# Layer 0 of a four-layer network on Trainium2: other operands and other engines for some of its work

## The chip, the cores and the metric

The kernel runs on one core of a Trainium2 chip. A core has a matrix engine (TensorE, PE in the profile, with its weight loads shown apart as PEld), three engines for elementwise work (VectorE or DVE, ScalarE or ACT, GpSimd or POOL), and SyncE (SP), which here only issues transfers. Each engine works through its own list of instructions in order and waits at semaphores for the others. Data lie in an on-chip memory (SBUF) of 128 partitions, in eight banks of an accumulation memory (PSUM), which PE writes, and in DRAM, which only DMA transfers reach. The metric is the device time of one execution of the whole program, in microseconds (us).

## The reference

Four layers are applied to an image x of 1 x 1024 channels x 64 x 64 pixels in float32, each as x + layer(groupnorm(x)). Layers 1 and 3 are 1x1 convolutions, layer 2 is a larger block with a selective scan. The change concerns layer 0 alone:

```
x_norm = layernorm2d(_gn(x), ln_w, ln_b)          # per channel, over 64 x 64 pixels
A_cont = -exp(log_A)                              # one per image row, 64
dt     = softplus(einsum('bsdc,c->bsd', x_norm, dt_w[0]) + dt_b[0])
log_a  = dt * A_cont                              # (channel s, image row d)
cums   = cumsum(log_a, axis=1)
M      = exp(cums[t] - cums[j]) for t >= j, else 0
out    = einsum('btjr,bjrc->btrc', M, x_norm)     # x = x + out
```

The channels are the sequence. For each channel and image row there is one dt: a weighted sum over the 64 pixels of that row. With a = exp(dt·A_cont), `out` is the recurrence out[t] = a[t]·out[t−1] + x_norm[t] along the 1024 channels, for every pixel, with one a for all pixels of an image row.

## The kernel before

**Tiles.** The image has channels on partitions when it arrives: 8 channel tiles of 128 x 4096 pixels. Layer 0 takes them in four pairs (`CH` = 2 channel tiles), and each pair in two halves of 32 image rows; that makes `NU` = 8 units. Unit u is pair u // 2, half u % 2. A unit is split into four pieces (`NPIECE`), so there are `NI` = 32 pieces. A piece is 512 pixels of the two channel tiles. In the turned layout, in which the recurrence runs, a tile has 128 pixels on the partitions (32 image rows x `TW` = 4 pixels) and the 256 channels of the pair along the free axis; a unit has `T0` = 16 such tiles, a piece has 4 of them.

**One unit's way.** `norm_chunk` works out mean and variance of a pair of channel tiles. `normalize(n)` (L580 to L587) makes a tile of 128 channels x 1024 pixels on ACT, with scale and bias per channel; there are 32 of them, four per unit, two of which feed two pieces. They have two buffers for each channel tile. `turn_in(i)` (L594 to L610) turns a piece: PE transposes (L602) into PSUM, and DVE (L608) or ACT (L610) writes it from there to `XT[i]` with the layernorm's weights. `row_dt(i)` (L612 to L618) adds the piece's part to the unit's row sums: the weights `dtm[:, t, :]` are stationary and the turned pixels move, so that PSUM gets the row sum of every pixel's row on all 128 partitions, as 128 x 256 channels. `decay(u, 0)` works out softplus on ACT (L627 to L630), as max(v, 0) + ln(1 + exp(−|v|)), in two tiles; `decay(u, 1)` adds the two by identity matmuls (L633); `decay(u, 2)` takes exp with the scale A to get the decays (L637 for the first channel, L638 for the others, spread over two tiles). `begin(u)` (L641 to L646), on POOL, adds what the last channel pair of the same half left to the first channel of the unit. `scan(i)` (L653) is the recurrence on DVE, two instructions of 512 for a piece. `hand_on(i)` (L658), on POOL, keeps the last channel. `turn_back(i)` turns a piece back (PE transposes, L679), and `add_up(i)` adds it to the image on DVE (L692), which also gives the sums for the next layer's statistics. Where `by_act(i, k)` holds (L660: pieces 25 to 30, second channel tile), PE adds the image itself by an identity matmul (L671, and products L677 in place of the transposes), and ACT copies the sum out (L690). `squares` (L704) gives the sums of squares on ACT.

**The order.** The whole layer is issued under a manual schedule: each engine gets its instructions in the order in which the program issues them. In the main loop, step i issues: the normalize of tile i+9, `decay(u+1, 1)` in the third step of a unit, `scan(i)`, `hand_on(i)`, `add_up(i−1)`, `turn_in(i+7)` (`LEAD` = 7), `row_dt(i+6)`, `turn_back(i)`, in a unit's second step `decay(u+1, 0)`, in its third `decay(u+1, 2)` and `begin(u+1)`, then pieces of the statistics, squares, a store of half the finished pair (`keep`, 2 MB, at steps 4, 12, 20, 28), the load of the last unit pair's first half at step 5 (`bring(6)`), and one turn of `sums`.

**The sums.** `sums` is work for later layers: `sum_weights` (L442 to L462) makes sums and differences of blocks of the two next weight matrices, in eight chunks. Chunk c loads four tiles of 256 KB (L450) at step 4c, does four POOL operations of 128x512 (L456 to L459) at step 4c+2, and stores four tiles (L462) at step 4c+3. Its transfers are issued by POOL, on its own DMA queue. The image's loads, the keeps and the weights of layer 1 are issued by SP.

Of the kernel before, what the change touches and what calls it, by code (L numbers as in the profile page):

```python
# [10 lines left out]
F32 = mybir.dt.float32  # L11
# [3 lines left out]
AF = mybir.ActivationFunctionType  # L15
ALU = mybir.AluOpType
# [4 lines left out]
P = 128  # L21
# [16 lines left out]
NK = -(-N // LT)  # L38
# [8 lines left out]
W1, WX, WR, WG, WO, W3 = range(6)  # L47
# [18 lines left out]
T0 = HN // P  # L66
TR = HW // 2
TW = HW // T0
# [6 lines left out]
        ("Alog", S), ("D", 1), ("mob", 4 * HEADS), ("dbcb", HEADS * NF)]  # L75

_CST = [("ident", P), ("fold", LC), ("same", P), ("upto", LC), ("far", LC), ("eye", LC), ("eye8", S),
        ("from", 1), ("to", NK), ("group", P), ("row", P),
        ("gx", NT), ("gy", NT), ("flip", 7)]


# [13 lines left out]
def tile_net(ctx: ExitStack, tc: tile.TileContext, x, par_d, cst_d, w_d, w2_d, dbcw_d, out):  # L95
# [28 lines left out]
    def pcol(name, i, rows=P):  # L124
        at = PAR[name].start + i
        return par[:rows, at : at + 1]
# [384 lines left out]
    with tc.issue_after(exp_ln.ins), tc.tile_pool(name="l0x", bufs=2) as lx, \  # L511
# [32 lines left out]
        nc.scalar.activation(negA0, par[:, PAR["logA"]], AF.Exp)  # L544
        negA = const.tile([P, S], F32, name="negA")
        nc.scalar.activation(negA, par[:, PAR["Alog"]], AF.Exp)
        dtm = l0.tile([P, T0, P], F32, name="dtm", bufs=1)
        for t in range(T0):
            nc.gpsimd.tensor_scalar(dtm[:, t, :], cst[:, CST["row"]], pcol("dtw", t), None, ALU.mult)
        carry = l0.tile([P, 2, T0], F32, name="carry", bufs=1)  # L550
# [29 lines left out]
        def normalize(n):  # L580

            u, j = divmod(n, 4)
            q, k = divmod(j, CH)
            scale, bias = norms[u // 2]
            xn[n] = l0.tile([P, 2, TR, HW // 4], F32, tag=f"xn{k}", name=f"xn{n}")
            part = half(u)[:, k, :].rearrange("p (r a g w) -> p a g r w", r=TR, a=2, g=2)[:, q]
            nc.scalar.activation(xn[n], part, AF.Identity, bias=bias[:, k : k + 1], scale=scale[:, k : k + 1])  # L587

        def tile_in(u, t, k):
            v = xn[4 * u + CH * (t // 8) + k].rearrange("p g r w -> p (g r w)")  # L590
# [21 lines left out]
        def row_dt(i):  # L612
            u, g = divmod(i, NPIECE)
            if g == 0:
                PD[u] = ps0.tile([P, FB], F32, tag="pd", name=f"pd{u}")
            for j in range(4):
                t = 4 * g + j
                nc.tensor.matmul(PD[u][:, : CH * P], dtm[:, t, :], XT[i][:, j, :], start=(t == 0), stop=(t == T0 - 1))  # L618

        def decay(u, step):  # L620

            if step == 0:
                e = l0.tile([P, CH * P], F32, tag="e", name=f"e{u}", bufs=1)
                m = l0.tile([P, CH * P], F32, tag="m", name=f"m{u}", bufs=1)
                dt[u] = e, m
                v = PD[u][:, : CH * P]
                nc.scalar.activation(e, v, AF.Abs, bias=pcol("dtb", 0))  # L627
                nc.scalar.activation(e, e, AF.Exp, scale=-1.0)
                nc.scalar.activation(m, v, AF.Relu, bias=pcol("dtb", 0))
                nc.scalar.activation(e, e, AF.Ln, bias=1.0)  # L630
            elif step == 1:
                for i, v in enumerate(dt[u]):
                    nc.tensor.matmul(PD[u][:, CH * P :], ident, v, start=(i == 0), stop=(i == 1))  # L633
            else:
                v, scale = PD[u][:, CH * P :], negA0[:, u % 2 : u % 2 + 1]
                if u > 1:
                    nc.scalar.activation(first_[u % 2], v[:, :1], AF.Exp, scale=scale)  # L637
                nc.scalar.activation(spread[u % 2][:, :, 1:], v[:, 1:].unsqueeze(1).to_broadcast([P, 2, CH * P - 1]),  # L638
                                     AF.Exp, scale=scale)
# [18 lines left out]
                nc.gpsimd.tensor_copy(carry[:, u % 2, 4 * g : 4 * g + 4], XT[i][:, :, CH * P - 1])  # L658

        def by_act(i, k):  # L660
            return NI - LEAD <= i < NI - 1 and k == 1

        def pieces_of(i, k):
            u, g = divmod(i, NPIECE)
# [38 lines left out]
                junk = junk[:, :FB].rearrange("p (r w) -> p r w", r=TR)  # L703
            nc.scalar.activation(junk, part, AF.Square, bias=nmean0[:, ct : ct + 1], accum_out=sq0[:, ct, at : at + 1])  # L704

        sums = (None for m in (W1, WX) for _ in sum_weights(m, wsum0, nc.gpsimd, lag=(1, 0)))
        LEAD = 7
        scores = make_scores()
        for k in range(CH):
# [34 lines left out]
                later[i] = [pieces.pop(0) for _ in range(n)]  # L744
        for i in range(NI):
            u, g = divmod(i, NPIECE)
            if i > 1 and i + LEAD + 2 < 4 * NU:
                normalize(i + LEAD + 2)
            if u + 1 < NU and g == 2:
                decay(u + 1, 1)  # L750
            scan(i)
            hand_on(i)
            if i == 0:
                finish_of(chain)
                chain = iter(())
            if i > 0:
                add_up(i - 1)
            if i == 0:
                turn_in(5, (2, 3))
                turn_back(0)  # L760
                turn_in(6, (2, 3))
                row_dt(5)
            elif i + LEAD < NI:
                if i == 1:
                    row_dt(LEAD - 1)
                    turn_in(LEAD, (2, 3))
                    normalize(LEAD + 3)
                turn_in(i + LEAD, (2, 3) if i > 11 and i % 2 else ())
            if 0 < i <= NI - LEAD:
                row_dt(i + LEAD - 1)  # L770
            if i > 0:
                turn_back(i)
            if i == 0:
                normalize(LEAD + 1)
                normalize(LEAD + 2)
            if u + 1 < NU and g == 1:
                decay(u + 1, 0)
            if u + 1 < NU and g == 2:
                decay(u + 1, 2)
                if u > 0:  # L780
                    begin(u + 1)
            for v, n in later.get(i, ()):
                unit_stats(v, (n,))
            if i in (3, 11):
                chain = norm_chunk(2 if i == 3 else 3)
            next(chain, None)
            if i >= NPIECE and g < CH:
                squares(u - 1, g)
            if u == NU - 1 and 0 < g:
                for k in range(CH):  # L790
                    squares(u, k, g - 1)
            if g == 0 and u % 2 == 1:
                last_keep = keep(u // 2)
            if i == NPIECE + 1:
                bring(6)
            next(sums, None)
# [1014 lines left out]
def _constants():  # L1811
    c = np.zeros((P, NCST), np.float32)
    p, j = np.arange(P)[:, None], np.arange(P)[None, :]
    c[:, CST["ident"]] = p == j
    h, r = np.divmod(p, LC)
    t = np.arange(LC)[None, :]
    c[:, CST["fold"]] = r == t
    c[:, CST["same"]] = h == j // LC
    c[:, CST["upto"]] = (t < S) | (r <= t)
    c[:, CST["far"]] = np.where((r >= S) & (t >= S) & (t < r), FAR, 0)  # L1820
    c[:, CST["eye"]] = (r == t) & (r >= S)
    c[:KW, CST["eye8"]] = np.tile(np.eye(S), (KW // S, 1))
    c[:, CST["from"]] = HEADS * N + np.where(r < S, h * S + r, HEADS * S)
    c[:, CST["to"]] = HEADS * N + np.arange(NK)[None, :] * P + p
    c[:, CST["group"]] = (p // 32 == j // 32) / 32
    c[:, CST["row"]] = p // TW == j // TW
    s = 1 - 2 * ((np.arange(P)[:, None] >> np.arange(6)[None, :]) & 1)
    s[:, 5] = 1
    c[:, CST["flip"]] = np.concatenate([s[:, :1], -s[:, :1], s[:, :5] * s[:, 1:]], axis=1)
    lin = _side()  # L1830
    c[:, CST["gx"]] = np.tile(lin, HW).reshape(NT, P).T
    c[:, CST["gy"]] = np.repeat(lin, HW).reshape(NT, P).T
    return c
# [63 lines left out]
```

## Time and profile before

| What | us |
|---|---|
| median of 3 runs | 2649.37 (2644.72 to 2649.58) |
| the profiled execution | 2649.3 |
| its span | 2647.4 |
| layer 0's steps 0 to 31, roughly | 42 to 203 |
| first matmul of layer 1 (L880) | 202.5 |
| one step while PE is without a gap (147 to 155 us) | 3.56 |

The mean clock that TensorE was granted is 0.993 of full speed. The profile's page gives busy time by engine; the trace behind it was asked for four stretches of layer 0, for what PE waited for, and for timelines. In a timeline a row has its start, its duration, the engine, the line of the program, the operation with output and inputs, the shape, the count of equal instructions in a row, and, in brackets, the idle time before it and what ended that. Since matmuls overlap, the distance between two starts tells more of PE's pace than the duration of a row.

### The profile page before, as it was taken

How to read it: one execution, taken by the hardware profiler on the slowest of the kernel's cores; microseconds unless marked ns; L12 is line 12 of the kernel's file. 1: busy time of each engine (PE TensorE's matmuls, PEld its weight loads, DVE VectorE, ACT ScalarE, POOL GpSimd, SP SyncE). 2: the span in 40 equal slices, each digit the busy share in tenths (PEclk: the TensorE clock that was granted, in tenths of full speed). 3: DMA queues.
4: the chain of work that ended last, by engine and by line, in shares of the span. 5: the costliest groups of instructions: out<-in, count | busy, mean ns of one | idle time of the engine just before them, and what ended most of it. 6: DMA issues, size and time to landing. Idle time of an engine off the chain costs nothing.

```text
span 2647.4 us, 30728 instructions
## 1 busy us (share of the span) xinstructions
PE 2561.7 (97%) x9588; PEld 1715.7 (65%) x9588; DVE 1817.3 (69%) x3794; ACT 1073.6 (41%) x1807; POOL 1225.4 (46%) x1142
## 2 busy tenths in 40 slices
PE   5889999999999999999999999999999999899998
PEld 4774444444555555544454548888888888788887
DVE  7986775674565554377877766576585775877877
ACT  4882110104655544476767662332233223312120
POOL 2464214322324142246464735575565665554544
PEclk9999999999999999999999999999999999999999
DMA  6555648656655676587677847899899898888896
GB/s 247 191 186 179 217 162 269 211 147 208 191 146 142 159 180 167 171 259 223 201 237 233 294 141 211 221 275 292 234 294 255 248 305 222 274 294 300 296 325 215
DMA packets 422772, 597.22 MB, mean 226 GB/s; under 512 B 142004, under 2 KB 210739, under 8 KB 419540
## 3 DMA queue, kind: packets, MB, share of 16 engines
q1 hardware_dynamic: 298052, 367.89, 44.4%
q10 hardware_dynamic: 91456, 136.33, 14.6%
q0 software_dynamic: 33104, 91.04, 13.5%
q8 instruction: 78, 1.28, 0.2%
q14 instruction: 82, 0.67, 0.1%
HBM read 435.10 MB, written 160.05 MB: 225 GB/s over the span
## 4 chain that ended last, share of the span: by engine, by line
PE 84%; DVE 6%; ACT 6%; DMA 1%; issue 1%; POOL 1%; SPq 0%; DVEq 0%; ACTq 0%; POOLq 0%
PE mm L880 38%; PE q_P2P L1771 5%; PE q_P6P L1771 5%; PE q_P5P L1771 5%; PE q_P3P L1771 5%; PE q_P7P L1771 5%; PE q_P4P L1771 5%; PE q_P1P L1771 5%; PE l2pt L1133 2%; PE py L1418 2%; ACT b L984 1%; DVE cvp L1114 1%; PE pd L618 1%; DVE xt L653 1%; PE pr L1379 1%
## 5 line engine op out<-in xcount | busy, mean ns | idle before, releaser
L880 PE MATMUL mm<-t,w 128*128 128x512 f32 x1536 | 681.4, 594 | 0.0
L880 PE MATMUL mm<-b,w 128*128 128x512 f32 x1152 | 513.2, 596 | 4.0 <-ACT b L984 2.9
L880 PEld LDWEIGHTS mm<-t,w 128*128 128x128 f32 x1536 | 286.0, 190 | 321.6 <-issue 314.6
L880 PEld LDWEIGHTS mm<-b,w 128*128 128x128 f32 x1152 | 215.4, 191 | 251.3 <-issue 239.0
L1427 POOL DMA_INDIRECT y_rows<-g,dst x74 | 73.6, 994 | 184.0 <-ACT g L1423 170.4
L1114 DVE SCALAR_TENSOR_TENSOR cvp<-xs,par,cvp 128x512 f32<-128x512 f32 x128 | 95.3, 754 | 78.9 <-ACT cvp L1111 76.7
L1740 ACT COPY qQ<-q_P5P 128x512 f32<-128x512 f32 x48 | 28.1, 585 | 294.0 <-PE q_P5P L1771 241.5
L470 POOL TENSOR_TENSOR s<-s 128x256 f32<-128x256 f32 (+3 forms) x120 | 130.2, 1090 | 7.5
L1421 ACT COPY g<-py 8x512 f32<-8x512 f32 x146 | 83.9, 575 | 107.4 <-PE py L1418 103.8
L1165 DVE TENSOR_TENSOR xs<-mm,xs 128x512 f32<-128x512 f32 x64 | 41.8, 685 | 119.0 <-PE mm L880 119.0
L1141 POOL TENSOR_TENSOR acc<-l2xt,acc 128x136 f32<-128x136 f32 x56 | 29.2, 522 | 193.6 <-ACT l2xt L1135 186.5
L1001 DVE SCALAR_TENSOR_TENSOR image<-mm,par,image 128x512 f32<-128x512 f32 x64 | 47.1, 746 | 87.7 <-PE mm L880 87.7
L1133 PEld LDWEIGHTS l2pt<-both,cv 128*128 128x128 f32 x512 | 77.4, 192 | 35.1 <-issue 22.7
L984 ACT ACTIVATE b<-image,gnl_bias,gnl_r_r 128x512 f32<-128x512 f32 x48 | 36.9, 808 | 144.1 <-PE mm L880 130.3
L1539 ACT ACTIVATE qb<-x_x_b,gn_bias,gn_r_r 128x512 f32<-128x512 f32 x64 | 48.8, 807 | 112.0 <-DVE qQ L1701 47.9
L1771 PE MATMUL q_P4P<-t_t,wq_P4P 128*128 128x256 f32 x384 | 92.5, 384 | 1.4 <-DVE qV L1748 1.4
L1771 PE MATMUL q_P1P<-t_b,wq_P1P 128*128 128x256 f32 x384 | 91.5, 382 | 1.5 <-POOL t_b L1535 1.5
L1535 POOL TENSOR_TENSOR t_t<-qt 128x512 f32<-128x512 f32 x23 | 29.6, 1288 | 135.9 <-DVE qt L1535 76.1
L838 POOL TENSOR_TENSOR t<-t,b 128x512 f32<-128x512 f32 x40 | 55.7, 1420 | 78.2 <-DVE t L838 78.1
L1748 DVE TENSOR_TENSOR qV<-q_P4P,qV 128x512 f32<-128x512 f32 x96 | 64.9, 686 | 38.7 <-PE q_P4P L1771 37.0
L1771 PE MATMUL q_P5P<-t_t,wq_P5P 128*128 128x256 f32 x384 | 90.8, 379 | 0.0
L1771 PE MATMUL q_P6P<-t_t,wq_P6P 128*128 128x256 f32 x384 | 90.7, 379 | 0.0
(433 smaller groups left out, 5991.4 us busy)
## 6 DMA issues: line engine op xcount, KB each, us to landing
w<-s_d SPq DMA_DIRECT2D x96, 512.0 KB
w<-in_w_dram SPq DMA_DIRECT2D x72, 512.0 KB
x_x_b<-x_d ACTq DMA_DIRECT2D x28, 1024.0 KB
image<-x_d SPq DMA_DIRECT2D x12, 2048.0 KB
wq_P6P<-s_d SPq DMA_DIRECT2D x84, 256.0 KB
wq_P7P<-s_d SPq DMA_DIRECT2D x84, 256.0 KB
wq_P5P<-s_d SPq DMA_DIRECT2D x84, 256.0 KB
wq_P3P<-s_d SPq DMA_DIRECT2D x84, 256.0 KB
```

What stands on the lines that cost most here:

```text
L470: eng.tensor_tensor(out, a, b, ALU.subtract)
L838: eng.tensor_tensor(B[name][k], B[one][k], B[two][k], ALU.subtract)
L880: nc.tensor.matmul(to[o], w[:, k, o * P : (o + 1) * P], B[name][k], start=(fresh and k == 0), stop=(k == KH - 1), skip_group_check=True)
L984: nc.scalar.activation(t, X[nb][:, ct, :], AF.Identity, bias=bias, scale=scale)
L1114: nc.vector.scalar_tensor_tensor(cv, xo[:, at + t : at + t + FB], pcol("dww", 3 * o + t), cv, ALU.mult, ALU.add)
L1133: nc.tensor.matmul(pt[:, q * NV : (q + 1) * NV], cv[:, (q0 + q) * P : (q0 + q + 1) * P], both[:, o, :], start=True, stop=True)
L1418: nc.tensor.matmul(py, G2[k % 2], rows[k][:, :DH], start=True, stop=True)
L1421: nc.scalar.copy(rows[k + 1][h * LC : h * LC + S, :DH], py[h * LC : h * LC + S])
L1427: nc.gpsimd.indirect_dma_start(out=y_views[k % len(y_views)][:, :], out_offset=bass.IndirectOffsetOnAxis(ap=dst_[:, k : k + 1], axis=0), i ...
L1539: nc.scalar.activation(tile_of(j, name)[:, k], held[j, "x", name][:, k], AF.Identity, bias=bias, scale=scale)
L1748: nc.vector.tensor_tensor(to, ps, to, ALU.add)
L1771: nc.tensor.matmul(ps[:, o, :], w[:, k, o * P : (o + 1) * P], rhs[:, k, :], start=(new and o == 0 and k == 0), stop=(k == 1), skip_group_c ...
```

## The change

Six things are changed, all in layer 0.

1. `row_dt`: the turned pixels are the stationary operand now, in two blocks of 128 channels, and `dtm`, which has 32 columns (one for each image row) in place of 128, moves. A piece has eight matmuls of 32 columns in place of four of 256. PSUM gets channels on the partitions and image rows along the free axis, 128 x 64 for a unit.
2. `decay`: |v| and exp work on 128 x 64; max(v, 0) and ln write 128 x 256, with each row's value repeated for its four pixels. `decay(u, 1)` adds the two parts and turns them to pixels on partitions in the same matmuls, four of 128 columns in place of two of 256.
3. `normalize` runs on POOL from tile 11 on (21 of 32 tiles), as one tensor_scalar with a multiplication and an addition; ACT keeps the first 11. In the loop they are issued in pairs at odd steps.
4. The sums' transfers are issued by SP in place of POOL.
5. `by_act` holds for pieces 4 to 13 too.
6. `turn_in` at odd steps from 13 on writes all four tiles by ACT; before, DVE wrote two of them.

```diff
-        ("from", 1), ("to", NK), ("group", P), ("row", P),
+        ("from", 1), ("to", NK), ("group", P), ("row", TR),
...
-        dtm = l0.tile([P, T0, P], F32, name="dtm", bufs=1)
+        dtm = l0.tile([P, T0, TR], F32, name="dtm", bufs=1)
...
-            nc.scalar.activation(xn[n], part, AF.Identity, bias=bias[:, k : k + 1], scale=scale[:, k : k + 1])
+            scale, bias = scale[:, k : k + 1], bias[:, k : k + 1]
+            if n > LEAD + 3:
+                nc.gpsimd.tensor_scalar(xn[n], part, scale, bias, ALU.mult, ALU.add)
+            else:
+                nc.scalar.activation(xn[n], part, AF.Identity, bias=bias, scale=scale)
...
-                nc.tensor.matmul(PD[u][:, : CH * P], dtm[:, t, :], XT[i][:, j, :], start=(t == 0), stop=(t == T0 - 1))
+                for k in range(CH):
+                    nc.tensor.matmul(PD[u][:, k * TR : (k + 1) * TR], XT[i][:, j, k * P : (k + 1) * P], dtm[:, t, :],
+                                     start=(t == 0 and k == 0), stop=(t == T0 - 1), skip_group_check=True)
...
-                e = l0.tile([P, CH * P], F32, tag="e", name=f"e{u}", bufs=1)
-                m = l0.tile([P, CH * P], F32, tag="m", name=f"m{u}", bufs=1)
+                f = l0.tile([P, CH, TR], F32, tag="f", name=f"f{u}", bufs=1)
+                e = l0.tile([P, CH, TR, TW], F32, tag="e", name=f"e{u}", bufs=1)
+                m = l0.tile([P, CH, TR, TW], F32, tag="m", name=f"m{u}", bufs=1)
                 dt[u] = e, m
-                v = PD[u][:, : CH * P]
-                nc.scalar.activation(e, v, AF.Abs, bias=pcol("dtb", 0))
-                nc.scalar.activation(e, e, AF.Exp, scale=-1.0)
-                nc.scalar.activation(m, v, AF.Relu, bias=pcol("dtb", 0))
-                nc.scalar.activation(e, e, AF.Ln, bias=1.0)
+                v = PD[u][:, : CH * TR].rearrange("p (k r) -> p k r", k=CH)
+                nc.scalar.activation(f, v, AF.Abs, bias=pcol("dtb", 0))
+                nc.scalar.activation(f, f, AF.Exp, scale=-1.0)
+                nc.scalar.activation(m, v.unsqueeze(3).to_broadcast([P, CH, TR, TW]), AF.Relu, bias=pcol("dtb", 0))
+                nc.scalar.activation(e, f.unsqueeze(3).to_broadcast([P, CH, TR, TW]), AF.Ln, bias=1.0)
             elif step == 1:
-                for i, v in enumerate(dt[u]):
-                    nc.tensor.matmul(PD[u][:, CH * P :], ident, v, start=(i == 0), stop=(i == 1))
+                for k in range(CH):
+                    for i, v in enumerate(dt[u]):
+                        nc.tensor.matmul(PD[u][:, (CH + k) * P : (CH + k + 1) * P], v[:, k].rearrange("p r q -> p (r q)"), ident,
+                                         start=(i == 0 and k == 0), stop=(i == 1), skip_group_check=True)
...
-            return NI - LEAD <= i < NI - 1 and k == 1
+            return (NPIECE <= i < 14 or NI - LEAD <= i < NI - 1) and k == 1
...
-        sums = (None for m in (W1, WX) for _ in sum_weights(m, wsum0, nc.gpsimd, lag=(1, 0)))
+        sums = (None for m in (W1, WX) for _ in sum_weights(m, wsum0, nc.sync, lag=(1, 0)))
...
-            if i > 1 and i + LEAD + 2 < 4 * NU:
+            if i > 1 and i % 2 and i + LEAD + 2 < 4 * NU:
                 normalize(i + LEAD + 2)
+                normalize(i + LEAD + 3)
...
                     normalize(LEAD + 3)
+                    normalize(LEAD + 4)
-                turn_in(i + LEAD, (2, 3) if i > 11 and i % 2 else ())
+                turn_in(i + LEAD, ())
```

More of the change, by code (lines that the diff above doesn't have):

```diff
@@ L1825, in _constants @@
     c[:, CST["group"]] = (p // 32 == j // 32) / 32
-    c[:, CST["row"]] = p // TW == j // TW
+    c[:, CST["row"]] = p // TW == np.arange(TR)[None, :]
     s = 1 - 2 * ((np.arange(P)[:, None] >> np.arange(6)[None, :]) & 1)
```

## The prediction

> **What bounds the kernel now.** I read the page's busy times first, then a table of the four stretches of layer 0, then what TensorE (PE) waited for there, then timelines of the places that the change touches.
>
> ```profile
> PE 2561.7 (97%) x9588; PEld 1715.7 (65%) x9588; DVE 1817.3 (69%) x3794; ACT 1073.6 (41%) x1807; POOL 1225.4 (46%) x1142
> ```
>
> PE is busy for 97% of the span. Nothing after layer 0 is edited, and PE is dense there; so the change is worth what it does to the moment at which PE leaves layer 0, at 202.5 us (the first L880 matmul). The stretches of layer 0, with columns from:to, length, busy PE, PEld, DVE, ACT, POOL, granted clock, DMA share, GB/s:
>
> ```profile
> 42.00:73.00 31.00, 25.20 (x142) 21.31 (x141) 26.63 (x53) 22.68 (x38) 10.39 (x16) 0.94 0.18 61
> 73.00:127.00 54.00, 43.42 (x256) 38.32 (x256) 49.84 (x98) 44.10 (x75) 22.74 (x44) 0.94 0.54 200
> 127.00:176.00 49.00, 46.84 (x299) 42.34 (x300) 47.27 (x89) 45.51 (x77) 29.87 (x56) 1.00 0.42 150
> 176.00:203.00 27.00, 17.30 (x88) 11.82 (x87) 20.05 (x53) 17.92 (x40) 13.32 (x24) 0.83 0.81 290
> ```
>
> From 127 to 176 us (steps 13 to 22 of 32) PE is the pacer: in the timeline below a step takes 3.56 us without a gap, and about 0.9 us is lost per four steps, at the decay. From 73 to 127 us (steps 4 to 13 or so) PE loses 10.6 us in eight gaps, and DVE is nearly full. The largest waits of PE from 72 to 126 us (total, times, longest; behind them come two of 2.3 and 2.0 us on the chain of the norm):
>
> ```profile
> PE xpt L602 <- ACT xt L610: 4.4, 4, 1.8
> PE pd L633 <- ACT e L630: 3.3, 2, 2.4
> ```
>
> One cycle of four steps in the PE-paced stretch, first PE, then POOL:
>
> ```profile
> 143.88 0.70 PE L633 MATMUL pd<-e,cst 128*128 128x256 f32 x2 [0.93 <-ACT e L630]
> ...
> 145.79 1.89 PE L618 MATMUL pd<-xt,dtm 128*128 128x256 f32 x8
> 147.52 1.04 PE L679 MATMUL pb<-cst,xt 128*128 128x128 f32 x8
> ...
> 155.56 1.13 PE L602 MATMUL xpt<-cst,xn 128*128 128x128 f32 x8
> ```
> ```profile
> 149.08 0.33 POOL L643 TENSOR_SCALAR carry<-carry,first 128x16 f32<-128x16 f32 x1 [2.40 <-PE xpt L602]
> ...
> 150.09 1.27 POOL L456 TENSOR_TENSOR s_s<-s_a,s_a 128x512 f32<-128x512 f32 x1
> ...
> 154.16 1.28 POOL L459 TENSOR_TENSOR s_a<-s_a,s_a 128x512 f32<-128x512 f32 x1
> ```
>
> The decay's turn starts at t0 = 143.88; PE reaches the turn_in of three steps later at 155.56, which is t0+11.68. POOL does begin, then a chunk of sums from 150.09 to 155.44 (5.35 us).
>
> **The change, part by part.**
>
> Turned pixels stationary (row_dt). Eight instructions of 32 columns, each two passes, replace four of 256. Before, a pass takes (147.52−145.79)/8 = 0.217 us, a piece 1.73. After it has 16 passes, each with its own load of a 128x128 f32 tile. No row shows 32 columns; the nearest is 64:
>
> ```profile
> 1243.38 0.35 PEld L1380 LDWEIGHTS pr<-ds,cst 128*128 128x128 f32 x2
> 1243.54 0.33 PE L1380 MATMUL pr<-ds,cst 128*128 128x64 f32 x2
> 1243.65 0.19 PEld L880 LDWEIGHTS mm<-b,w 128*128 128x128 f32 x1
> ```
>
> The second load of L1380 starts at 1243.54 by its own record, L880's at 1243.65: successive loads stand 0.11 us apart, beside passes of only 64 columns, and this is the pace of a 128-column transpose too (eight from 147.52 to 148.40, where the next group starts). I take 0.11: 16×0.11 = 1.76 against 1.73, no change. Ends: 0.055, half of it, if a 32-column pass hides half of its load; 0.137, if its 27 ns (0.217×32/256) come on top.
>
> Decay. Step 1 becomes eight passes of 128 columns, 0.88 for 0.87: nothing. Abs and Exp go from 256 to 64 columns (488 and 417 ns; a one-column ACT row, L637, is 262), so about 0.35 us goes from the chain that ends at the turn; Relu and Ln write as much as before. At the first decay, before 73 us, it is on the path: −0.4. The 16 dtm builds on POOL (9.36 us from 7.37) get shorter, but end long before the first use at 27.3: nothing.
>
> Early additions by TensorE and ACT (steps 4 to 13, one tile of each piece). The late pieces show the price: an identity matmul of 512 columns in two passes and four f32 products stand in place of four transposes.
>
> ```profile
> 178.61 1.06 PE L677 MATMUL pb<-cst,xt 128*128 128x128 f32 x8
> 179.51 1.02 PE L671 MATMUL pb<-low,cst 128*128 128x512 f32 x2
> 180.37 0.60 PE L679 MATMUL pb<-cst,xt 128*128 128x128 f32 x4
> ```
>
> By starts, 0.90+0.86+0.44 = 2.20 us against 0.88 (147.52 to 148.40): +1.3 us of PE per piece, ten pieces, +13.0. In 73 to 127 us PE works 54.1−10.6 = 43.5 us; with 13.0 it is 56.5, already +2.4. DVE loses 10×0.76 = 7.6 us there (L692, 0.68+0.08) and ACT gains ten rows of L690 (0.59+0.19, 7.8 us) while it loses its normalizes; ACT has room for that. Of the 10.6 us of waits, the two of the norm's chain (4.3 by the waits' rows, of which 2.4 lie in gaps that no other work of PE fills) and about 1.5 of the rest I keep: 3.9. One more stretch at half clock, as the rows 0.94 and 0.83 show follows idle PE, 0.7; POOL's lateness (next part) about 1.0. 56.5+3.9+0.7+1.0 = 62.1, +8.1 against 54.1. Ends: +2.4 (no wait is left) to +13 (all are).
>
> Late normalizes on POOL. 21 tiles 128x1024, 1.24 us each on ACT (L587), go to POOL as two-operation tensor_scalars in pairs at odd steps, needed two steps later. No such row exists. POOL's tensor_scalar with one operation and 128 columns takes 9.36/16 = 0.585; a copy of 1024 columns, without arithmetic, takes 1.04:
>
> ```profile
> 7.37 9.36 POOL L549 TENSOR_SCALAR dtm<-cst,par 128x128 f32<-128x128 f32 x16 [6.26 <-DMA cst<-in_cst_dram]
> ...
> L1276 POOL COPY both<-cst 128x1024 f32<-128x1024 f32 x1 | 1.0, 1040 | 30.6 <-DMA s_d<-s 30.6
> ```
>
> A tensor_scalar of two columns (L551) keeps POOL for 0.18 (16.70 to 16.88, the next one's start); 0.405/126 per further column gives 3.5 us for 1024, and the slope from the 16-column row L643 (0.33) gives 2.6. I take 3.05, between the two of its own kind. Ends: the copy's 1.04, and 8×0.585 = 4.7; two L456 rows of 512 columns, with two inputs, would be 2.5.
>
> What is queued behind it: POOL works in order, and the pair of step 4c+3 stands behind begin and the whole chunk. `first` now ends a normalize earlier (148.64+0.26−1.13 = 147.77, t0+3.9); begin ends at t0+5.0, the chunk at t0+10.4, the pair at t0+10.4+6.1 = t0+16.5. PE reaches the transposes that read it at t0+11.7: a stall of 4.8, less the 0.35 by which the turn starts earlier: 4.45. It comes at steps 17 and 21: +8.9. (In steps 4 to 13 PE is slower by 3×1.3 by then, reaches it at t0+15.6, and loses 0.9 at two places, of which I count half: the 1.0 above.) Ends: 1.04 gives (12.5−11.7−0.35)×2 = +0.9; 2.5 gives +6.7; 4.7 gives (19.8−11.7−0.35)×2 = +15.5.
>
> The sums' transfers on SP's queue. 64 DMA issues leave POOL, with 28.2 us of waits for landings of stores. What stood behind them was begin of the last unit, and behind that a scan:
>
> ```profile
> 181.24 1.60 POOL L450 DMA_DIRECT2D s_a<-in_w_dram  x3 [0.97 <-DMA s_d<-s_a]
> 182.88 0.34 POOL L643 TENSOR_SCALAR carry<-carry,first 128x16 f32<-128x16 f32 x1
> ```
> ```profile
> 183.53 1.23 DVE L653 TENSOR_TENSOR_SCAN xt<-a,xt 128x512 f32<-128x512 f32 x1 [3.94 <-POOL xt L646]
> ```
>
> `first` was there at 178.16, begin could start only at 182.88. Now SP does this waiting: −3.9. On SP the loads stand behind the keeps' 2 MB and the last image tile; behind the sums stand layer 1's first weights. I cost that at nothing: a chunk has two steps (7 us) between load and use, and the weight that waits longest, behind chunk 7's stores, is used some 14 us after layer 0's end. If that cover is gone, each us of lateness costs one. Ends: −3.9 to +3.
>
> Evictions. Six odd steps move two 128x256 evictions from DVE (0.54) to ACT (0.57): ACT gets 6.8 us from step 13 on, and the normalizes take off over 14 us of it there: nothing.
>
> Sum: −0.4+8.1+8.9−3.9 = +12.7. The profiled execution took 2649.3 us (span 2647.4), the median 2649.37; so 2662.
>
> [...]
>
> **The rivals.** (1) Other side: a 32-column pass is far cheaper than a load of 0.11. At 0.055 row_dt costs 0.88 less per piece: 10 steps give −8.8, the two cycles to 176 us give no more than −1.7 because POOL then sets them, and about −5 before 73 us: 2662−15.5 = 2646.5. It turns to faster at a pace near 0.06. For it: nothing but overlap of loads; against it: L1380's loads.
> (2) POOL's normalize is as quick as its copy, 1.04: +0.9 for +8.9, and no lateness in steps 4 to 13 (−1.0): 2653. For it: L1276; against: L549.
> (3) DVE, 49.8 busy of 54, and not PE sets 73 to 127 us; losing 7.6 it ends 6 earlier: 2648. Against: PE's work alone is then 56.5.
> (4) Two operations take 4.7 or more on POOL: +15.5 there, and the second pair of a cycle is late too, 2 each: 2669 to 2673.
>
> **How the numbers follow.** The forecast 0.48, rival 1 0.13, rival 2 0.15, rival 3 0.10, rival 4 0.14. The range 2647 to 2673 leaves out about half of rival 1, some of 3 and the far end of 4. A measurement tells 0.2% (5.3 us) from nothing: faster lies below 2644.1, slower above 2654.7. Rivals 1 and 3 are split between faster and same, rival 2 between same and slower. Faster 0.14, same 0.15, slower 0.71.
>
> **What would show it.** Of each step: the passes of row_dt start 0.11 us apart (rival 1: 0.055); steps 4 to 13 take about 4.9 us with a 512-column identity matmul in each; the normalize rows on POOL last about 3.05 us, and PE's transposes wait for POOL at steps 17 and 21 for some 4.5 us; no scan waits for POOL at the last begin; DVE is down by 14 us and ACT by over 10. It would be wrong above all if the POOL tensor_scalar of 1024 columns is much quicker than its rows of 128 say, or if SP's queue delivers a chunk or a weight late.

## The result, and the profile after

The changed kernel takes 2657.45 us (median of 18), the kernel before 2648.31 us (median of 18 runs on the same chips): ratio 1.0042, 95% interval 1.0032 to 1.0052. It is slower by about 9 to 11 us, in the range that was predicted and on the side that was predicted. The profiled execution takes 2662.3 us (span 2660.5), 13 us more than the one of before. Of the 18 runs eight took 2661.8 us or more, the profiled one among them, and ten 2657.7 or less. The page's busy times after:

```profile
PE 2589.4 (97%) x9936; PEld 1751.7 (66%) x9936; DVE 1809.5 (68%) x3762; ACT 1059.5 (40%) x1818; POOL 1210.9 (46%) x1099
```

PE has 27.7 us more busy time and its loads (PEld) 36.0; DVE has 7.8 less, ACT 14.1 and POOL 14.5. The first matmul of layer 1 starts at 216.16 us (202.54 before); from there to the end it takes 2444.3 us (2444.8 before). So all of it lies in layer 0, as the prediction assumed. Within layer 0, though, it is split quite otherwise. The table takes the start of the first scan of a step as a mark.

| Stretch | before, us | after, us | difference | predicted |
|---|---|---|---|---|
| to the first scan | 42.42 | 49.57 | +7.15 | −0.4 |
| scan 0 to 4 | 30.47 | 31.68 | +1.21 | (in the −0.4) |
| scan 4 to 14 | 52.11 | 57.24 | +5.13 | +8.1 |
| scan 14 to 26 | 48.84 | 51.39 | +2.55 | +8.9 |
| scan 26 to 31 | 18.22 | 14.69 | −3.53 | −3.9 |
| scan 31 to layer 1 | 10.48 | 11.59 | +1.11 | 0 |
| sum | | | +13.62 | +12.7 |

The stretches of the changed kernel, with the columns as in the prediction (from:to, length, busy PE, PEld, DVE, ACT, POOL, granted clock, DMA share, GB/s), cut at or near scans 0, 4, 14 and 26:

```profile
49.57:81.00 31.43, 29.22 (x192) 28.23 (x191) 26.03 (x50) 18.60 (x35) 9.28 (x11) 0.89 0.09 34
81.00:140.00 59.00, 56.17 (x384) 49.86 (x384) 44.23 (x80) 38.35 (x81) 25.29 (x38) 0.88 0.49 178
140.00:190.00 50.00, 47.50 (x410) 45.88 (x409) 41.41 (x76) 40.25 (x80) 28.84 (x45) 1.00 0.48 167
190.00:216.00 26.00, 17.76 (x111) 13.04 (x110) 22.66 (x43) 18.97 (x43) 9.60 (x12) 0.90 0.72 253
```

PE is busy for 56.17 of 59 us about scan 4 to 14, near the forecast's 56.5, but partly at a lower rate: the granted clock is 0.88 there, where before it was 0.94. The largest difference stands ahead of the first scan. Here is the timeline of PE after:

```profile
27.42 3.46 PE L623 MATMUL pd<-dtm,xt 128*128 128x32 f32 x16
30.69 1.95 PE L606 MATMUL xpt<-cst,xn 128*128 128x128 f32 x8
32.43 3.46 PE L623 MATMUL pd<-dtm,xt 128*128 128x32 f32 x16
...
37.45 6.87 PE L623 MATMUL pd<-dtm,xt 128*128 128x32 f32 x32
```

And before:

```profile
27.50 3.11 PE L618 MATMUL pd<-xt,dtm 128*128 128x256 f32 x8
30.44 1.11 PE L602 MATMUL xpt<-cst,xn 128*128 128x128 f32 x8
31.40 1.89 PE L618 MATMUL pd<-xt,dtm 128*128 128x256 f32 x8
```

The same eight transposes take 0.96 us before (30.44 to 31.40) and 1.74 us after (30.69 to 32.43). Sixteen passes of row_dt take 3.27 us after (27.42 to 30.69), 0.213 us for most of them, where 0.11 was priced. All of PE runs at half its rate here. Before, that ends at 29.6 us; after, at 57.1. The column of the granted clock does not tell it: it shows 1.00 for 20 to 42 us in both kernels (first before, then after). The pace of the passes does.

```profile
20.00:42.00 22.00, 15.79 (x74) 13.44 (x74) 17.20 (x41) 11.16 (x17) 0.00 (x0) 1.00 0.86 356
20.00:42.00 22.00, 18.38 (x88) 18.05 (x87) 14.78 (x34) 7.08 (x10) 0.00 (x0) 1.00 0.99 403
```

I call a pass half-rate when its start and the next one's stand 0.21 to 0.22 us apart for 32 or 128 columns (0.11 at the full rate) or 0.42 to 0.44 for 256 (0.22), and add up such passes from 20 us to layer 1. Before it is 14.7 us, after 43.3 us (within 24 to 58, 66 to 74, 84 to 91, 94 to 102 us). Half of the difference, 14 us, is time that the same passes would not have taken at full rate.

### The profile page after: what moved, and what is told of

Its sections match the earlier page's. It is cut to its first block, busy times and chain, and to the rows that moved or that the text cites. A ratio compares the mean times of both kernels' runs of the same rounds, so it can differ in the third digit from the quotient of the medians.

```text
span 2660.5 us, 31438 instructions
## 1 busy us (share of the span) xinstructions
PE 2589.4 (97%) x9936; PEld 1751.7 (66%) x9936; DVE 1809.5 (68%) x3762; ACT 1059.5 (40%) x1818; POOL 1210.9 (46%) x1099
## 3 DMA queue, kind: packets, MB, share of 16 engines
q0 software_dynamic: 27984, 74.26, 11.7%
## 4 chain that ended last, share of the span: by engine, by line
PE 86%; DVE 6%; ACT 4%; issue 1%; DMA 1%; POOL 1%; SPq 0%; DVEq 0%; ACTq 0%; POOLq 0%
PE mm L891 39%; PE q_P2P L1782 5%; PE q_P3P L1782 5%; PE q_P5P L1782 5%; PE q_P1P L1782 5%; PE q_P7P L1782 5%; PE q_P6P L1782 5%; PE q_P4P L1782 5%; PE l2pt L1144 2%; PE py L1429 2%; PE pd L623 2%; PE xpt L606 1%; ACT b L995 1%; DVE cvp L1125 1%; PE pr L1390 1%
## 5 line engine op out<-in xcount | busy, mean ns | idle before, releaser
L1550 ACT ACTIVATE qb<-x_x_b,gn_bias,gn_r_r 128x512 f32<-128x512 f32 x64 | 48.8, 807 | 110.1 <-DVE qQ L1712 36.0
L1546 POOL TENSOR_TENSOR t_t<-qt 128x512 f32<-128x512 f32 x23 | 29.6, 1287 | 135.8 <-DVE qt L1546 68.8
```

## Experiments

Theory A: row_dt's passes of 32 columns cost no more than their loads, but while they run so few columns stream through TensorE that its clock falls, or does not rise, and everything on PE pays. Theory B, the prediction's: row_dt is neutral; the additions on TensorE and POOL's late normalizes make the loss.

**Only row_dt undone.** The changed kernel with row_dt, `dtm` and decay as in the kernel before:

```diff
-                for k in range(CH):
-                    nc.tensor.matmul(PD[u][:, k * TR : (k + 1) * TR], XT[i][:, j, k * P : (k + 1) * P], dtm[:, t, :],
-                                     start=(t == 0 and k == 0), stop=(t == T0 - 1), skip_group_check=True)
+                nc.tensor.matmul(PD[u][:, : CH * P], dtm[:, t, :], XT[i][:, j, :], start=(t == 0), stop=(t == T0 - 1))
```

> The changed kernel with row_dt, dtm and decay as before (turned pixels move, 256 columns); the rest of the change stays. Theory (clock): in the changed kernel's trace the passes of TensorE stand 0.21 us apart from 24 to 57 us, in the trace of before only to 30 us; the 32-column passes are what keeps it slow. Then the first scan comes at about 42.5 us in place of 49.6, and the time is 7 to 9 us under the changed kernel's, about 2649, ratio to before 0.999 to 1.002. Rival (the prediction's own term: row_dt neutral; the late start has another cause, such as the transfers on SP's queue): first scan stays near 49.6, ratio about 1.004.

Measured: 2649.12 us, ratio 1.0008 (1.0000 to 1.0017). (Line numbers of the experiments' kernels differ by a few from those of after.) The first scan starts at 42.04 us, half-rate time is 10.0 us. Nearly the whole loss goes with row_dt, as theory A has it.

**Only row_dt changed.** The kernel before with the same part alone.

> The kernel before with only row_dt, dtm and decay changed. Theory (clock): first scan near 49.6 us, passes 0.21 us apart until about 57 us; time about 7 us over before, ratio 1.002 to 1.004. Rival (neutral, as predicted): first scan near 42, ratio 0.999 to 1.001.

Measured: 2656.59 us, ratio 1.0039 (1.0024 to 1.0053): this part alone costs what the whole change costs. The profiled execution took 2648.7 us, the least of its six timed runs (up to 2660.5), and there the first scan comes at 42.22, against the expectation. In this profile the passes of 32 columns do come to the full rate at the start:

```profile
27.39 2.46 PE L619 MATMUL pd<-dtm,xt 128*128 128x32 f32 x16
29.69 1.19 PE L602 MATMUL xpt<-cst,xn 128*128 128x128 f32 x8
...
33.45 3.66 PE L619 MATMUL pd<-dtm,xt 128*128 128x32 f32 x32
38.47 0.49 PE L637 MATMUL pd<-cst,e 128*128 128x128 f32 x2 [1.36 <-ACT e L633]
38.79 0.56 PE L637 MATMUL pd<-cst,m 128*128 128x128 f32 x2
39.15 0.64 PE L637 MATMUL pd<-cst,e 128*128 128x128 f32 x2
```

The first sixteen take 2.30 us (27.39 to 29.69). PE falls to half rate only behind the wait of 1.36 us (two passes in 0.42 us from 39.15), and the half rate comes at other places than in the changed kernel (most of it at 43 to 52, 77 to 93, 121 to 134 us), 41.2 us in all. It also costs less: layer 1 starts at 205.44 us, 2.9 us later than before, and PE still has 7.2 us of gaps from scan 4 to 14, against 10.1 before and 2.6 in the changed kernel. So where PE runs at half rate, and what that costs, differs from one profile to the other, though the passes up to the first scan are the same. The time goes with the part; the place of the loss in one profile need not be that of another. That also limits the table above: its +7.15 is one execution's.

**Work added.** The changed kernel with wide matmuls where PE waits for the first normalized tile:

```diff
+        warm = ps0.tile([P, FB], F32, tag="pd", name="warm")
+        for _ in range(5):
+            nc.tensor.matmul(warm, ident, cst[:, :FB], start=True, stop=True)
         turn_in(0, range(4))
```

> The changed kernel plus five extra identity matmuls of 512 columns, into a PSUM tile that nobody reads, put before the first turn_in, where TensorE waits from about 20 to 23 us: work added, nothing taken away. Theory (clock follows how much streams through TensorE): the first transposes already run at 0.11 to 0.12 us a pass, row_dt at 0.11, the first scan comes 5 to 8 us earlier than 49.6, and the time falls by 4 to 8 us against the changed kernel, to about 2650 to 2653. Rival (the late start is the cost of the instructions themselves or of something else than the clock): nothing earlier, time 2657 or up to 1 us more. A case between: it is quick at first and falls back to 0.21 in row_dt, then 1 to 3 us are gained.

Measured: 2657.19 us, ratio 1.0038 (1.0025 to 1.0051), no gain in time. PE's timeline:

```profile
19.77 6.49 PE L728 MATMUL warm<-cst 128*128 128x512 f32 x10
26.09 2.08 PE L606 MATMUL xpt<-cst,xn 128*128 128x128 f32 x16
28.01 1.87 PE L623 MATMUL pd<-dtm,xt 128*128 128x32 f32 x16
...
33.48 3.66 PE L623 MATMUL pd<-dtm,xt 128*128 128x32 f32 x32
38.50 0.80 PE L641 MATMUL pd<-cst,e 128*128 128x128 f32 x2 [1.36 <-ACT e L637]
39.09 0.63 PE L641 MATMUL pd<-cst,m 128*128 128x128 f32 x2
```

The added matmuls bring the full rate ahead of the transposes: these 16 take 1.92 us (26.09 to 28.01), row_dt runs at 0.11 a pass, and the first scan starts at 42.38 (in the profile of row_dt alone it starts at 42.22 without them). But after 32 passes of 32 columns and a wait of 1.36 us PE is back at half rate (two passes in 0.42 us from 39.09), later again, 33.1 us in all. The rate, once reached, wasn't kept, and the added work is no remedy.

**The same passes with four times the columns.** This is the run that tells the form of the passes from the columns. `dtm` gets its 128 columns back and moves against the same stationary turned pixels; instructions and loads are as many as in the changed kernel.

```diff
-                    nc.tensor.matmul(PD[u][:, k * TR : (k + 1) * TR], XT[i][:, j, k * P : (k + 1) * P], dtm[:, t, :],
+                    nc.tensor.matmul(PD[u][:, k * P : (k + 1) * P], XT[i][:, j, k * P : (k + 1) * P], dtm[:, t, :],
...
-                v = PD[u][:, : CH * TR].rearrange("p (k r) -> p k r", k=CH)
+                v = PD[u][:, : CH * P].rearrange("p (k r q) -> p k r q", k=CH, q=TW)[:, :, :, 0]
```

> The changed kernel with dtm of 128 columns (each row's weight four times) moving against the same stationary turned pixels: the same number of instructions and weight loads, four times the columns; decay reads every fourth of them. Theory (the clock falls for want of columns that stream, not for the form of the passes): passes stay about 0.11 us at full rate, the half-rate time before layer 1 falls from over 33 us to 15 or less, the first scan comes at about 42.5, and the time falls by 5 to 8 us to about 2650, though more is streamed. Rival (the swap of operands itself, a new load for each pass, is what costs): time as the changed kernel's, 2657, or over it.

Measured: 2647.28 us, ratio 1.0010 (1.0001 to 1.0019), against 1.0042 with 32 columns. Half-rate time 11.3 us.

```profile
27.42 2.10 PE L623 MATMUL pd<-dtm,xt 128*128 128x128 f32 x16
29.36 1.12 PE L606 MATMUL xpt<-cst,xn 128*128 128x128 f32 x8
...
33.08 3.74 PE L623 MATMUL pd<-dtm,xt 128*128 128x128 f32 x32
38.17 0.49 PE L641 MATMUL pd<-cst,e 128*128 128x128 f32 x2 [1.36 <-ACT e L637]
38.50 0.39 PE L641 MATMUL pd<-cst,m 128*128 128x128 f32 x2
```

Row for row this begins as the changed kernel does, at 27.42. Here the rate doubles within the first sixteen passes. That alone tells nothing, as it came with 32 columns too, in row_dt alone; but it also outlasts the 1.36 us wait at 38.17, behind which it fell in both profiles above (it falls later, from 41.6 to 44.7 us). Four times the columns cost nothing (0.112 us a pass at full rate with 32 and with 128), 0.3% comes back in the timed runs, and half-rate time falls from 43.3 us to 11.3. That the columns decide, and not the form of the passes, is shown by this pair.

**The additions back on DVE.** First in the changed kernel:

```diff
-            return (NPIECE <= i < 14 or NI - LEAD <= i < NI - 1) and k == 1
+            return NI - LEAD <= i < NI - 1 and k == 1
```

> The changed kernel with the additions of pieces 4 to 13 back on DVE. Theory: TensorE sets the stretch of steps 4 to 13 and the additions cost it 1.3 us a piece; from scan 4 to scan 14 the time falls from 57.2 to about 50 to 53 us (52.1 before the change), total 4 to 7 us under the changed kernel, about 2651 to 2653. Rival (DVE sets this stretch as in the kernel before, and the additions on TensorE relieve it): no gain or a loss, 2657 to 2660.

Measured: 2653.19 us, ratio 1.0028 (1.0018 to 1.0038): some 4 us by the medians, with intervals that overlap slightly. Its profile can't be read by stretches: it has 65.5 us of half rate, and scan 4 to 14 took 51.8 us in spite of it. Then the same with row_dt undone as well, where the clock is quiet:

> The changed kernel with both undone: row_dt and decay as before, and the additions of pieces 4 to 13 back on DVE. What is left of the change: late normalizes on POOL, the sums' transfers on SP, the evictions by ACT. Theory: the additions cost TensorE some 4 us here too, and what is left is worth its -3.5 at the last begin; the time falls 4 to 7 us under that of the kernel with only row_dt undone, to about 2642 to 2645, ratio to before 0.998 to 0.9995. Rival (the additions relieve DVE where it sets the pace once the clock is not lost): same as with them, ratio 1.000 to 1.002.

Measured: 2646.28 us, ratio 1.0003 (0.9994 to 1.0012), not told apart from 1.0008 with the additions. In the traces scan 4 to 14 takes 48.6 us without them and 51.95 with them: the additions cost 3.35 us in this stretch. But 48.6 is 3.5 us less than before the change, so that stretch as a whole loses nothing while the clock holds. ACT is busy for 33.3 us there, where before it was 42.7; DVE for 48.2 and 47.9. What is gained there is lost in scan 14 to 26 (53.5 us against 48.8), with 1.8 us of waits for POOL's tiles, 1.9 in the norm's chain and a half-rate stretch from 122 to 126 us among it. The evictions by ACT were run only together with the late normalizes, so what they cost alone isn't known.

**The normalizes on POOL at twice the work.** On the kernel with only row_dt undone:

```diff
-                nc.gpsimd.tensor_scalar(xn[n], part, scale, bias, ALU.mult, ALU.add)
+                nc.gpsimd.tensor_scalar(xn[n], part, scale, None, ALU.mult)
+                nc.gpsimd.tensor_scalar(xn[n], xn[n], bias, None, ALU.add)
```

> The kernel with only row_dt undone, and each late normalize on POOL done as two instructions (multiplication, then addition), which doubles its time to about 2.4 us. By the prediction's own arithmetic the pair then ends at t0+10.4+4.9 = t0+15.3 and TensorE, which reaches it at t0+11.7, waits about 3.6 us at steps 17 and 21 in place of 0.8 to 1.2: +5 to +6 us against the kernel with only row_dt undone, about 2654 to 2655. Rival (TensorE's order or POOL's gives more slack than the arithmetic): waits under 2 us, +0 to +2.

Measured: 2691.54 us, ratio 1.0173 (1.0158 to 1.0189), over 40 us more than with one instruction, and not 6. First the group of POOL in the changed kernel (its columns: count, busy us, mean ns, idle before), then the groups of this one:

```profile
L589 POOL TENSOR_SCALAR xn<-image,gn_r_r,gn_bias 128x1024 f32<-128x1024 f32 x12 | 14.2, 1194 | 0.6 <-PE xpt L606 0.6
```
```profile
L590 POOL TENSOR_SCALAR xn<-xn,gn_bias 128x1024 f32<-128x1024 f32 x21 | 59.8, 2849 | 2.0
L589 POOL TENSOR_SCALAR xn<-image,gn_r_r 128x1024 f32<-128x1024 f32 x12 | 34.2, 2846 | 0.0
```

With both operations in one instruction 1024 columns take 1.19 us; with one operation, 2.85. Two instructions make 5.7 us a tile, and POOL has four tiles in four steps: 22.8, with begin 1.0, the chunk 5.4 and the copies 0.6 it is 29.8 us. The trace has 29.89 us from scan 18 to 22 and again from 22 to 26. POOL paces the layer here, and PE waits for it by 34.8 us in nine waits. The order of POOL's queue that the prediction worked with thus holds; it was the size of an instruction that was off, and it is here again: the expectation took 2.4 us a tile.

**Prices of POOL's tensor_scalar.** Ten of them on 896, 512, 128 and 32 columns, added to the kernel before where POOL is idle: for each size one with two operations (L560), one with one (L561), and at the end both with constants.

> The kernel before with ten tensor_scalars added on POOL right after the dtm builds, where POOL is idle: two operations (multiplication, addition) and one operation, scalars from memory, on 896, 512, 128 and 32 columns, then both with constants on 896. If the form decides, two operations on 896 take about 1.1 us and one operation about 2.5 (from 1.19 and 2.85 at 1024), with memory scalars and with constants alike; if the form with memory scalars is what is slow with one operation, the constants make it about 1.1. If the size or the place decides, both forms take the same at each size.

Measured, POOL's timeline:

```profile
17.26 1.07 POOL L560 TENSOR_SCALAR pr<-cst,par 128x896 f32<-128x896 f32 x1
18.43 2.53 POOL L561 TENSOR_SCALAR pr<-cst,par 128x896 f32<-128x896 f32 x1
...
23.59 0.44 POOL L560 TENSOR_SCALAR pr<-cst,par 128x128 f32<-128x128 f32 x1
24.12 0.60 POOL L561 TENSOR_SCALAR pr<-cst,par 128x128 f32<-128x128 f32 x1
24.83 0.36 POOL L560 TENSOR_SCALAR pr<-cst,par 128x32 f32<-128x32 f32 x1
25.28 0.36 POOL L561 TENSOR_SCALAR pr<-cst,par 128x32 f32<-128x32 f32 x1
25.73 0.94 POOL L562 TENSOR_SCALAR pr<-cst 128x896 f32<-128x896 f32 x1
26.76 2.45 POOL L563 TENSOR_SCALAR pr<-cst 128x896 f32<-128x896 f32 x1
```

The form decides: 1.07 against 2.53 us for 896 columns. With two operations a further column costs 0.82 ns ((1.07−0.36)/864), with one 2.5 ns, with scalars from memory and with constants alike. At 32 columns the two can't be told apart.

**The sums' transfers alone.** The kernel before, with `nc.sync` in place of `nc.gpsimd` in the line of `sums`.

> The kernel before with only the sums' transfers issued by SP. As predicted: the scan of 3.94 us of waiting at the last begin is gone, -3 to -4, ratio 0.9985 to 0.9990, if SP's queue delays nothing. Rival: chunk loads behind the keeps arrive late, or the first weights of layer 1 do, and the gain is given back: ratio 0.9995 to 1.001.

Measured: 2644.33 us against 2644.49, ratio 1.0000 (0.9991 to 1.0009). From scan 26 to 28 it takes 5.68 us in place of 9.69: the wait is gone as predicted. But the first matmul of layer 1 comes at 200.9, only 1.6 us sooner, which the interval of the timed runs doesn't tell from nothing. POOL, and then DVE, in the norm ahead of layer 1:

```profile
197.20 1.26 POOL L456 TENSOR_TENSOR s_s<-s_a,s_a 128x512 f32<-128x512 f32 x1 [11.82 <-DMA s_a<-in_w_dram]
198.54 1.27 POOL L457 TENSOR_TENSOR s_a<-s_a,s_a 128x512 f32<-128x512 f32 x1
```
```profile
197.55 0.93 DVE L173 TENSOR_TENSOR gnl_r_t<-gnl_r_r 128x8 f32<-128x8 f32 x1 [0.51 <-ACT gnl_r_r L171]
198.52 0.17 DVE L174 SCALAR_TENSOR_TENSOR gnl_r_t<-gnl_r_t,gnl_v 128x8 f32<-128x8 f32 x1
198.72 1.12 DVE L175 SCALAR_TENSOR_TENSOR gnl_r_r<-gnl_r_t,gnl_r_r 128x8 f32<-128x8 f32 x1
```

Operations on 128x8 take 0.17 us before, all five of this chain. Two of them now take 0.93 and 1.12, and end at 198.48 and 199.84, as POOL's operations end (198.46, 199.81). They begin while such an operation runs. The last chunk came late (POOL waited 11.82 us for its loads) and so fell into the norm. In the changed kernel it is one operation of 1.25 us.

**The loads ahead of the keep.** The sums' turn is issued before the 2 MB store in each step, the transfers still on SP.

> The kernel before with the sums' transfers on SP, and in each step the turn of sums issued ahead of the keep (a chunk's loads then stand before the 2 MB store on SP's queue). In the kernel with the transfers on SP alone, the last chunk's four POOL operations start at 197.2 us, and two 128x8 DVE operations of the norm that begins layer 1 take 0.93 and 1.12 us in place of 0.17, each ending with a POOL operation. Theory (the loads came late behind the keep, and POOL's 128x512 operations hold DVE's operations with two inputs in SBUF): the last chunk's operations start 4 to 7 us earlier, the norm's DVE operations take 0.17 each, the first matmul of layer 1 comes at about 199, ratio 0.998 to 0.999. Rival (the loads are late for another cause, such as the stores that free their tiles): chunk still in the norm, ratio 0.9995 to 1.0005.

Measured: 2651.10 us, ratio 1.0016 (1.0007 to 1.0025), slower. The last chunk starts 3.8 us earlier, and norm operations still take 0.93, 0.66 and 1.12 us. What costs more is the next in the queue, by the waits of PE:

```profile
PE mm L880 <- DMA w<-in_w_dram: 8.0, 1, 8.0
```

Layer 1's first weights now stand behind the chunk and the keep, and its first matmul starts at 204.85. So the order on SP's queue has a price at both ends. The same order with the normalizes on POOL and the evictions by ACT:

> The kernel with late normalizes on POOL, evictions by ACT and the sums' transfers on SP (row_dt and the early additions as before), and the turn of sums ahead of the keep. Theory: the 1.0 us that a norm operation lost to POOL comes back, and the normalizes on POOL neither gain nor cost: ratio 0.999 to 1.000, no better than the sums alone. Rival (ACT's relief pays once nothing else stands in the way): 0.997 to 0.9985.

Measured: 2650.80 us, ratio 1.0010 (1.0002 to 1.0019), layer 1 starts at 205.6. That is no better than the same kernel with the other order (1.0003), and no gain from ACT's relief.

**The last chunk later.** Chunks 0 to 6 on SP, chunk 7 on POOL's queue behind a small copy that reads the norm's variance:

```diff
...
+        nc.gpsimd.tensor_copy(off, var1)
+        for _ in sums:
+            pass
```

> The kernel before with the transfers of chunks 0 to 6 of the sums on SP, and chunk 7 (loads, operations, stores) on POOL's queue, held by a small POOL copy that reads the variance of the norm after layer 0. Theory: the gain at the last begin (4.0 us from scan 26 to scan 28) stays only if nothing of the sums stands in the norm (0.17 us for each of its DVE operations) or before layer 1's first weights on SP's queue: first matmul of layer 1 at 198.5 to 199.5 us against 202.5, ratio 0.998 to 0.999. Rival (the start of layer 1 is bound by its weights whatever the order, or chunk 7 now late delays layer 1's sums): first matmul at 201 or later, or a wait for a weight behind it, ratio 0.9995 to 1.001.

Measured: 2642.80 us against 2645.01, ratio 0.9992 (0.9983 to 1.0001). In the profile the norm's operations take 0.17 us each, layer 1 starts at 197.4 us (202.5 before), and the span is 2640.5 (2647.4 before). Its ratio is the lowest of these kernels, and the median moves by 2.2 us; the interval still touches 1, so that a gain is likely but not settled. The profile's 5 us are more than the median shows, and 1.3 of them lie ahead of the first scan (41.11 against 42.42), where the two kernels do the same work.

## Why the prediction came out right, and where it was wrong

The time, the direction and the range hold. That the sum holds is luck, by two errors that cancel: row_dt was priced at nothing and costs 9 to 10 us, and with it undone the other parts cost 2.3 us together by the medians (2649.12 against 2646.84), where 8.1+8.9−3.9 = 13.1 was forecast.

- "Turned pixels stationary (row_dt)": "16×0.11 = 1.76 against 1.73, no change". The price of a pass at full rate was right: 0.112 us. The step failed all the same, since the price of the other passes isn't independent of it. The part costs 0.3 to 0.4% (undone 1.0008 in place of 1.0042, alone 1.0039), about what the whole change costs. The prediction allowed 0.7 us for "one more stretch at half clock", where this profile has about 14, and tied the half clock to idle PE; in the changed kernel PE is busy for 56.17 of 59 us at 0.88. The trace of before held a warning: it too ran at half rate from 24.5 to 29.6 us, where PE, after a wait of 3 us, was dense.
- "At the first decay [...] −0.4": +7.15 in this profile, for the same reason.
- "Early additions": +1.3 us of PE a piece is right in size (0.94, 0.90 and 0.44 us at full rate for the three groups of passes, less 0.88). Of +8.1 for the stretch +5.13 came, and with the clock intact the stretch takes 51.95 us against 52.11. In that stretch PE is then busy for 50.1 us (42.0 before), 8 more where 13 was priced, and its gaps fall from 10.1 us to 1.9, where I kept 3.9. The other parts relieve ACT, and the additions themselves cost 3.35.
- "Late normalizes on POOL", "I take 3.05": 1.19 measured, so 8.9 became two waits of 0.8 us each for POOL's tiles, and 2.55 in the stretch with the rest. By the prediction's arithmetic 1.19 gives 10.4+2.4−11.7−0.35 = 0.8 us a cycle, which is what the trace has:

```profile
PE xpt L606 <- POOL xn L589: 1.6, 2, 0.8
```

  So rival 2's condition held (its 2653 did not, for the clock's sake), and the failed term is the size: I priced an instruction with two operations from rows with one. For one operation 3.05 was near (2.85): a further column costs 2.5 ns with one operation and 0.82 with two.
- "The sums' transfers": −3.9, measured −3.53 at its place (−4.0 alone). "I cost that at nothing" failed: the last chunk came late and fell on the norm, +1.1 here, and the weights behind it pay when the order is turned. The norm's DVE operations take 0.17 us alone. In the changed kernel one of them with two inputs in SBUF (L174) begins 0.04 us after one of POOL's operations of 128x512 and takes 1.25: it ends at 214.86 us, as that one does (214.83). One with its input in PSUM (L217), wholly beside such an operation, takes 0.17. The scans, with one input in PSUM, show none of it: 1.16 to 1.22 us each in the changed kernel, beside POOL's operations or not.
- Rivals 1, 3 and 4 didn't come: passes of 32 columns stand 0.11 apart at full rate, the stretch from scan 4 to 14 didn't shrink in the changed kernel, and POOL was quicker, not slower. Against rival 3, with the old row_dt: taking the additions off DVE (48.2 us busy, then 43.3) makes the stretch 3.35 us longer; it shrinks, by 3.5, with DVE as busy as before and ACT relieved.

On the clock: in the changed kernel's profile PE issues passes from 24.15 to 44.3 us almost without a gap and stays at half rate until 57; in that of row_dt alone the same passes rise within 5 us, and with 128 columns within 4. So PE can be busy by the profile for 20 us and stay at half rate, and need not. What decides between the two, these runs do not settle.

## What to carry to other kernels

Matmuls that stream few columns per weight load can cost nothing at their own place and still slow the others: here passes of 32 columns stood 0.112 us apart at full rate, as those of 128 did, and TensorE ran at half its rate for 43.3 us before layer 1, against 11.3. So compare the pace of equal passes in the two traces, since busy time (56.17 of 59 us) and even the granted clock (1.00 from 20 to 42 us) did not show it here. Price an instruction from rows of exactly its form, the number of its operations included (896 columns on POOL took 1.07 us with two operations and 2.53 with one). And when transfers move to another queue, look for what then runs late at the end of the stage, and which short chain it will fall on.

## What the runs showed that I had not expected

- The rate of TensorE depended on the columns that stream: half-rate time before layer 1 was 10 to 16 us in the kernels with 128 or more columns in row_dt and POOL's normalizes in one instruction, and 33 to 66 us in the four profiles with 32. The mean granted clock of the timed runs agrees: 0.983 to 0.993 in the 41 runs with 32 columns, 0.991 or below in 39 of them; 0.991 to 0.995 in the 81 runs of the other experiments but the one that POOL paces, 0.992 or above in 74 of them.
- The timed runs of the 32-column kernels also spread more (2650 to 2666 us for the changed kernel, 2643 to 2652 for the one before). Within the changed kernel the eight longest show 0.991 to 0.993 and the ten others 0.988 to 0.990. That the longer runs have the higher figure fits a half rate at the start that this figure doesn't show, as in the profile; for the runs without a profile it isn't shown.
- GpSimd's tensor_scalar is 2.4 times slower with one operation than with two: 2.53 against 1.07 us for 896 columns.
- DVE operations of 128x8 with two SBUF inputs took up to 1.25 us in place of 0.17 beside GpSimd's operations of 128x512 on SBUF (1.25 in the changed kernel, 0.93 and 1.12 with the transfers alone moved).
